# Edge-gated graph layer: one look-ahead tile, edge sums in pairs, z kept in used-up sums, products spread over a block

## The chip, the core and the metric

The kernel runs on one core of one Trainium2 chip. Its time is the device time of one launch in microseconds; the number compared is the median over several runs. All data is float32. Engines are named as the profile names them: PE (matrix products; PEld are its weight loads), DVE (vector), ACT (scalar and activation), POOL (here it only issues indirect transfers), SP (issues plain transfers).

## The reference, cut to what matters

```python
B, N, D = 16, 1024, 256                 # batches, nodes, features
pre_u = x @ W1[:D]                      # (B, N, D), per source node u
pre_v = x @ W1[D:]                      # (B, N, D), per target node v
hidden = relu(pre_u[:, :, None, :] + pre_v[:, None, :, :] + b1)      # (B, u, v, D)
S   = sigmoid(hidden @ W2 + b2)         # (B, u, v), one gate for each pair
a_t = einsum('buv,bud->bvd', S * adj, x)        # gated sums over the sources
m_t = einsum('uv,bud->bvd', adj, x) * x         # plain sums, times x
z   = x + (a_t @ Wa + ba) + (m_t @ Wm + bm)     # beta1 = beta2 = beta3 = 1
```

`adj` is mostly zero: 9052 of its 1024 x 1024 entries are not, at most 19 in a column. Gates are needed only for those.

## The kernel before, in words

**Edges, tiles, steps.** The kernel lists the edges and works on them alone. The 16 batches form 4 groups g of GB = 4; the 1024 targets form 8 tiles vt of 128. A pair (g, vt) is a *block*, 32 in all (`order`). A block has two windows w of 64 targets, and each window's edges lie in TW = 5 *edge tiles* j of up to 128 edges, one on each partition. So a block has T = 10 steps and the kernel 320; step n handles edge tile n, and s = n mod 10 is its place in the block. Targets of a window form four quarters of 16; edge tile j holds edges of one quarter (j = 0, 4) or of two (j = 1, 2, 3) (`QUARTERS`).

**What a tile needs.**
- `fetch(n)` (L494-499): POOL issues an indirect transfer which brings for each of the 128 edges the row of its source node from `table[g]`: 8 KB, the 4 x 256 values of pre_u and the 4 x 256 values of x. It goes into buffer `fetched[n % 6]`.
- `expand(n)` (L564-570): PE multiplies a 0/1 matrix (`marks`) with pre_v + b1 (`cuts`), which gives each edge the row of its target: 128 x 1024 in PSUM, tile `pc`, two buffers.
- `gate(n)` (L598-612): DVE adds both into the SBUF tile `t`, one buffer (L601); four DVE instructions, one for each batch, take relu, multiply by W2 and sum (L606); ACT makes the sigmoid (L609) and four copies (L612) that scale the one-hot adjacency columns by the gate. They fill the gated half of `lefts[n]`.
- `left_adj(n + 1)` (L573-580): ACT writes the ungated half of the next tile's `lefts`, a copy for each of the four batches.
- `aggregate(n)` (L614-625): PE multiplies `lefts` with the fetched x (L623). Each product uses 32 columns of the array, 16 targets gated and 16 ungated, and four batches fill 128. It adds up in `acc0` and `acc1`. `half_end` copies a finished pair of quarters to SBUF with ACT (L631).

**What a block needs besides.** `halves` (L452-468): pre_v of the next block on PE (L427, L431), its split into high and low parts on ACT and DVE (L461-468). `rows` (L434-446): pre_u of a block on PE, which SP writes to `table`. Group 0's table is made before the loop, the others inside it, each ahead of the group's use; the last `rows` are at step 233. `turn_over` (L633-657): transposes the sums on PE (L641), copies them on ACT into `LT` (L644), and two steps later DVE multiplies the ungated half by x (`times_h`, L654). `block_end` (L659-680): four pieces of products with Wa and Wm (L672), ACT copies them to `z` (L675), DVE adds x two steps later (L676), SP sends `z` out three steps after the last piece (L678). `lists(vt)` makes the edge lists; four of eight run inside the loop, their DVE instructions strewn between the gates by `fill`.

**Order.** All five queues are written by hand (`manual_schedule`): the order of the calls in the loop is the order on each engine, and the framework adds only the semaphore waits. `after(step, f)` puts f into a table that `do(step)` empties. A step before is, in this order:

```python
aggregate(n - 1); fetch(n - 1 + NF)            # NF = 6
gate(n); left_adj(n + 1)
do(n)
expand(n + 2)
# then transfers, lists, and the products of the block:
#   turn_over at s = 7 (two), 9, and 1 of the next block; block_end at s = 3, 4, 5, 6
#   halves at s = 0, 2, 3, 5, 6; rows by a table of steps (mostly s = 8 and 1)
```

Of the kernel before, what the change touches and what calls it, by code (L numbers as in the profile page):

```python
# [7 lines left out]
FP = mybir.dt.float32  # L8
# [5 lines left out]
P = 128  # L14
# [3 lines left out]
def kernel(  # L18
# [196 lines left out]
    wk = main.enter_context(tc.tile_pool(name="wk", bufs=3))  # L215
    psc = main.enter_context(tc.tile_pool(name="psc", bufs=2, space=bass.MemoryType.PSUM))
# [12 lines left out]
    NF = 6  # L229
# [9 lines left out]
    def lists(vt):  # L239
        key = fetched[vt + 1][:, :N] if vt < EARLY else big.tile([P, N], FP, name="key", bufs=1)  # L240
        (nc.sync if 2 <= vt < EARLY else nc.gpsimd).dma_start(key, adjT[vt * P:(vt + 1) * P, :])
        yield "load"
        R = wk.tile([P, RC], FP, name="R", bufs=4)
        top = R[:, 5:5 + S]
        count = wk.tile([P, 1], FP, name="count", bufs=4)
        unread = one.tile([P, N], mybir.dt.uint8, name="unread")
# [9 lines left out]
        cand = wk.tile([P, N // P, 8], FP, name="cand", bufs=2)  # L256
# [5 lines left out]
        cut = wk.tile([P, 1], FP, name="cut", bufs=2)  # L262
# [12 lines left out]
        used = wk.tile([P, S], FP, name="used", bufs=4)  # L275
# [14 lines left out]
        from_ = wk.tile([P, 1], FP, name="from", bufs=4)  # L290
# [9 lines left out]
        held = wk.tile([P, 1], FP, name="held", bufs=4)  # L300
# [10 lines left out]
        mark = big.tile([P, E], FP, name="made", bufs=1)  # L311
        nc.vector.tensor_scalar(mark, slot, R[:, 0:1], None, ALU.is_lt)
        yield "op"
        none = wk.tile([P, 1], FP, name="none", bufs=4)
# [6 lines left out]
        last = wk.tile([P, 1], FP, name="last", bufs=4)  # L321
# [4 lines left out]
        RR = wk.tile([P, NW, RC], FP, name="RR", bufs=2)  # L326
        few = wk.tile([P, E], mybir.dt.uint8, name="few", bufs=2)
# [13 lines left out]
        L = wk.tile([P, M, RC], FP, name="L", bufs=2)  # L341
# [3 lines left out]
        s_of = wk.tile([P, M], FP, name="s_of", bufs=2)  # L345
        nc.vector.tensor_tensor(s_of, slot_of.rearrange("p w j -> p (w j)"), L[:, :, 1], ALU.subtract)
        yield "op"
        eq = wk.tile([P, M, S], FP, name="eq", bufs=1)
# [5 lines left out]
        k_of = wk.tile([P, M], FP, name="k_of", bufs=2)  # L354
# [139 lines left out]
    def fetch(n):  # L494
        k, g, vt, w, j = where(n)
        nc.gpsimd.indirect_dma_start(  # L496
            out=fetched[n % NF], out_offset=None, in_=table[g],
            in_offset=bass.IndirectOffsetOnAxis(ap=uidx[:, vt * NW + w, j:j + 1], axis=0),
            bounds_check=N - 1, oob_is_err=False)
# [73 lines left out]
    def left_adj(n):  # L573
# [4 lines left out]
        lefts[n] = wk.tile([P, 2, GB, 2, V], FP, name="left")  # L578
        nc.scalar.activation(lefts[n][:, :m, :, 0, :], onehot[:, i, o:o + m, :].unsqueeze(2).to_broadcast([P, m, GB, V]),  # L579
# [17 lines left out]

    def gate(n):  # L598
        k, g, vt, w, j = where(n)
# [344 lines left out]
```

## Time and profile before

| | us |
|---|---|
| median of 3 runs (1163.63, 1163.78, 1171.99) | 1163.78 |
| the profiled execution: span | 1165.8 |
| first tile's DVE add (L601) starts | 71.6 |
| step 110 starts, by the same line | 480.8 |
| step 240 | 897.6 |
| step 319, the last | 1145.4 |
| busy in the span: PE / DVE / ACT / POOL | 1092.1 / 1056.2 / 893.5 / 439.9 |

A step starts here where DVE starts its add. The profiled execution is one of its own; it is 2 us longer than the median. PE's busy time is made of modelled ends of pipelined products, so what PE can spare is read from the distances between the starts of its products. The transfer engines (16, shared by all queues) move 391 MB in the span, 300 MB of it the indirect fetches.

### The profile page before, as it was taken

The page shows a single profiled execution, that of the slowest core. Times are in us where ns is not written, and L with a number is a line of the kernel's source. Part 1 is how long each engine was busy: PE and PEld are TensorE (multiplying, and loading weights), DVE is VectorE, ACT ScalarE, POOL GpSimd, SP SyncE. Part 2 cuts the span into 40 slices and gives each one's busy share as a digit, 9 for nine tenths or more (in the row PEclk, how much of TensorE's full clock was granted, in tenths as well). Part 3 has the DMA queues.
Part 4 walks back from the last instruction along what each step waited for, and adds up shares of the span by engine and source line. Part 5 has one row for each costly group of instructions (what it writes and reads, how often), then busy time and mean ns, then how long its engine had stood idle before and what let it go on. Part 6 is the DMA issues. An engine that isn't in the chain of part 4 may idle for free. (4 is left out here: it accounts for less than half of the span.)

```text
span 1165.8 us, 23918 instructions
## 1 busy us (share of the span) xinstructions
PE 1092.1 (94%) x7633; PEld 723.1 (62%) x7633; DVE 1056.2 (91%) x3487; ACT 893.5 (77%) x2624; POOL 439.9 (38%) x428
## 2 busy tenths in 40 slices
PE   7867899999999999999999999999999999999986
PEld 6744666666666666666666666666666666666553
DVE  7688889888999989999999999999999999999994
ACT  2346587767887878888888888888888888888873
POOL 1556645253335333443333333333333333333330
PEclk9868899999999999999999999999999999999999
DMA  9986898999999999999999999999998998999991
GB/s 286 298 307 223 277 372 312 362 320 331 342 320 323 396 379 336 358 350 402 389 374 369 355 364 356 360 364 383 371 375 324 361 322 333 334 339 328 328 346 60
DMA packets 147048, 391.40 MB, mean 336 GB/s; under 512 B 16753, under 2 KB 105329, under 8 KB 110705
## 3 DMA queue, kind: packets, MB, share of 16 engines
q0 software_dynamic: 50016, 300.50, 68.9%
q1 hardware_dynamic: 81616, 74.99, 20.0%
q10 hardware_dynamic: 15280, 14.29, 3.7%
q8 instruction: 63, 1.03, 0.3%
q14 instruction: 73, 0.59, 0.1%
HBM read 393.78 MB, written 50.33 MB: 381 GB/s over the span
## 5 line engine op out<-in xcount | busy, mean ns | idle before, releaser
L496 POOL DMA_INDIRECT fetched<-table,uidx x320 | 341.5, 1067 | 628.3 <-PE acc L623 447.2
L606 DVE SCALAR_TENSOR_TENSOR t<-t,w_b 128x256 f32<-128x256 f32 x1280 | 478.3, 421 | 19.3 <-ACT left L612 0.5
L601 DVE TENSOR_TENSOR t<-fetched,pc 128x1024 f32<-128x1024 f32 x320 | 389.3, 1217 | 41.4 <-PE pc L569 13.9
L623 PE MATMUL acc<-fetched,left 128*32 128x256 f32 x4096 | 336.2, 391 | 31.9 <-ACT left L612 26.2
L612 ACT ACTIVATE left<-left,gt 128x32 f32<-128x32 f32 (+1 forms) x1280 | 299.3, 304 | 10.4
L569 PE MATMUL pc<-X,mark 128*128 128x512 f32 x640 | 237.6, 453 | 6.2 <-ACT mark L562 5.0
L623 PEld LDWEIGHTS acc<-fetched,left 128*32 128x32 f32 x4096 | 130.6, 109 | 179.3 <-issue 52.4
L569 PEld LDWEIGHTS pc<-X,mark 128*128 128x128 f32 x640 | 97.2, 191 | 140.0 <-issue 89.3
L609 ACT ACTIVATE gt<-sc,b_b 128x4 f32<-128x4 f32 x320 | 96.2, 301 | 43.4 <-DVE t L606 40.8
L672 PE MATMUL misc<-w_m,LT 128*128 128x256 f32 x496 | 117.2, 379 | 0.0
L672 PE MATMUL misc<-w_a,LT 128*128 128x256 f32 x496 | 117.1, 379 | 0.0
L579 ACT ACTIVATE left<-onehot,val 128x128 f32<-128x128 bf16 (+1 forms) x320 | 116.5, 364 | 0.0
L427 PE MATMUL misc<-w_v,hT 128*128 128x256 f32 x448 | 107.3, 383 | 0.0
L427 PE MATMUL misc<-w_u,hT 128*128 128x256 f32 x416 | 101.2, 390 | 5.7 <-ACT few L329 3.6
L606 DVE DVE_READ_ACCUMULATOR t<-t,w_b 128x1 f32 x1280 | 104.0, 81 | 0.0
L672 PEld LDWEIGHTS misc<-w_a,LT 128*128 128x128 f32 x496 | 93.9, 189 | 15.1
L672 PEld LDWEIGHTS misc<-w_m,LT 128*128 128x128 f32 x496 | 93.8, 189 | 14.9
L382 POOL DMA_INDIRECT val<-in_adjT_dram,vidx x80 | 85.7, 1071 | 35.1 <-issue 22.4
L427 PEld LDWEIGHTS misc<-w_v,hT 128*128 128x128 f32 x448 | 86.0, 192 | 13.9
L427 PEld LDWEIGHTS misc<-w_u,hT 128*128 128x128 f32 x416 | 79.5, 195 | 17.3 <-ACT few L329 3.7
L631 ACT COPY ev<-acc 128x512 f32<-128x512 f32 x128 | 75.5, 590 | 14.6 <-PE acc L623 4.2
L675 ACT COPY z<-misc 128x512 f32<-128x512 f32 x62 | 36.3, 586 | 58.1 <-PE misc L672 38.8
(164 smaller groups left out, 947.9 us busy)
## 6 DMA issues: line engine op xcount, KB each, us to landing
h_blk<-in_x_dram SPq DMA_DIRECT2D x31, 512.0 KB
out_dram<-z SPq DMA_DIRECT2D x31, 512.0 KB
hT<-in_xT_dram SPq DMA_DIRECT2D x28, 512.0 KB
table<-in_x_dram ACTq DMA_DIRECT2D x24, 512.0 KB
table<-tab SPq DMA_DIRECT2D x24, 512.0 KB
fetched<-table,uidx POOLq DMA_INDIRECT x320
table<-in_x_dram SPq DMA_DIRECT2D x8, 512.0 KB
table<-fetched SPq DMA_DIRECT2D x8, 512.0 KB
```

Of the source, the lines that this page charges most:

```text
L382: nc.gpsimd.indirect_dma_start(out=val[:, i, j:j + 1], out_offset=None, in_=adj_flat, in_offset=bass.IndirectOffsetOnAxis(ap=vidx[:, i, j: ...
L427: nc.tensor.matmul(p[:, bb * D:(bb + 1) * D], hT[:, 2 * h + bb, i, :], wt[:, i, :], start=(i == 0 and not begun), stop=(i == DC - 1), skip ...
L496: nc.gpsimd.indirect_dma_start(out=fetched[n % NF], out_offset=None, in_=table[g], in_offset=bass.IndirectOffsetOnAxis(ap=uidx[:, vt * NW ...
L569: nc.tensor.matmul(pcs[n][:, c], marks[n // TW][:, j * P:(j + 1) * P], cuts[k][:, w, c], start=True, stop=True)
L579: nc.scalar.activation(lefts[n][:, :m, :, 0, :], onehot[:, i, o:o + m, :].unsqueeze(2).to_broadcast([P, m, GB, V]), AF.Copy, scale=val[:, ...
L601: nc.vector.tensor_tensor(t, fetched[n % NF][:, :GD].rearrange("p (b d) -> p b d", b=GB), pcs.pop(n).rearrange("p (b d) -> p b d", b=GB), ...
L606: nc.vector.scalar_tensor_tensor(t[:, b, :], t[:, b, :], 0.0, w2_b, ALU.max, ALU.mult, accum_out=sc[:, b:b + 1])
L609: nc.scalar.activation(gt, sc, AF.Sigmoid, bias=b2_b)
L612: nc.scalar.activation(lefts[n][:, :m, b, 1, :], lefts[n][:, :m, b, 0, :], AF.Copy, scale=gt[:, b:b + 1])
L623: nc.tensor.matmul(accs[h][b * 2 * V:(b + 1) * 2 * V, r, :], left[:, i, b].rearrange("p k v -> p (k v)"), f[:, GD + b * D:GD + (b + 1) * D ...
L631: nc.scalar.copy(evs[q], accs.pop(q))
L672: nc.tensor.matmul(pz[:, bb * D:(bb + 1) * D], LTs[k][:, c, 2 * h + bb, i, :], wt[:, c, :], start=False, stop=(i == 0 and c == DC - 1), sk ...
```

## The change

- **Add ahead.** The DVE add is a function of its own, `add(n)`, and is issued a step early: step n issues `add(n + 1)`, then `gate(n)`. The sum goes into the first half of the fetched buffer itself; the tile `t` is gone.
- **Aggregate later, in pairs.** Step n issues `aggregate(n - 2)`. From step 110 on, even steps issue none and odd steps issue those of n - 3 and n - 2 one after the other. The last steps catch up.
- **Buffers.** Seven fetch buffers in place of six, and an eighth from step 110 on, when the tiles of the edge lists (now in a pool of their own, `lst`) are given back. A fetch takes whichever buffer became free first. `lefts` has five buffers in place of three, each smaller: the ungated columns are written twice in place of four times, each copy shared by two neighbouring batches, so that in batches 1 and 3 the ungated 16 columns come first.
- **z.** The tile `z` is gone. ACT copies the products into the part of `LT` that they have just used up, DVE adds into the loaded x block (`h_blk`) one step later in place of two, and SP sends `h_blk` out. The next block's `h_blk` has the same single buffer. `times_h` of the second window comes one step after its transposes, not two.
- **Products spread.** The transposes stand at s = 8, 9, 0, 2, and `rows` mostly at s = 8 and 9. Up to step 119 `expand(n + 2)` and the products of the block are issued ahead of `add` and `gate`, from step 120 on after them.

The diff, cut to its core:

```diff
-    NF = 6
+    NF = 7
+    at_slot, free = {}, list(range(NF))
...
+        at_slot[n] = free.pop(0)
         nc.gpsimd.indirect_dma_start(
-            out=fetched[n % NF], out_offset=None, in_=table[g],
+            out=fetched[at_slot[n]], out_offset=None, in_=table[g],
...
-        lefts[n] = wk.tile([P, 2, GB, 2, V], FP, name="left")
-        nc.scalar.activation(lefts[n][:, :m, :, 0, :], onehot[:, i, o:o + m, :].unsqueeze(2).to_broadcast([P, m, GB, V]),
+        lefts[n] = wk.tile([P, 2, 2 * GB - 1, V], FP, name="left", bufs=5)
+        nc.scalar.activation(lefts[n][:, :m, 1::GB, :],
+                             onehot[:, i, o:o + m, :].unsqueeze(2).to_broadcast([P, m, GB // 2, V]),
...
+    def add(n):
+        t = fetched[at_slot[n]][:, :GD]
+        nc.vector.tensor_tensor(t, t, pcs.pop(n), ALU.add)
+
     def gate(n):
-        t = one.tile([P, GB, D], FP, name="t")
-        nc.vector.tensor_tensor(t, fetched[n % NF][:, :GD].rearrange("p (b d) -> p b d", b=GB),
-                                pcs.pop(n).rearrange("p (b d) -> p b d", b=GB), ALU.add)
+        t = fetched[at_slot[n]][:, :GD].rearrange("p (b d) -> p b d", b=GB)
...
-        after(step + (1 if k == BS - 1 else 2), times_h)
+        after(step + (1 if k == BS - 1 or w else 2), times_h)
...
-            nc.scalar.copy(z[:, sl], pz.rearrange("p (b d) -> p b d", b=2))
-            after(step + 2, lambda sl=sl: nc.vector.scalar_tensor_tensor(z[:, sl], hb[:, sl], be1, z[:, sl],
-                                                                         ALU.mult, ALU.add))
-        after(step + 3, lambda: nc.sync.dma_start(
-            out[g * GB:(g + 1) * GB, vt * P:(vt + 1) * P, :].rearrange("b p d -> p b d"), z))
+            z = LTs[k][:, 2 * h].rearrange("p k c n -> p (k c n)").rearrange("p (b d) -> p b d", b=2)
+            nc.scalar.copy(z, pz.rearrange("p (b d) -> p b d", b=2))
+            after(step + 1, lambda sl=sl, z=z: nc.vector.scalar_tensor_tensor(hb[:, sl], hb[:, sl], be1, z,
+                                                                              ALU.mult, ALU.add))
+        after(step + 2, lambda: nc.sync.dma_start(
+            out[g * GB:(g + 1) * GB, vt * P:(vt + 1) * P, :].rearrange("b p d -> p b d"), hb))
...
-        if 1 <= n <= total:
-            aggregate(n - 1)
-            fetch_val(2)
-            if n - 1 + NF < total:
-                fetch(n - 1 + NF)
...
+    ROOM, MORE = 110, 1
+    ahead = NF
+    add(0)
+    def refill():
+        nonlocal ahead
+        while free and ahead < total:
+            fetch(ahead)
+            ahead += 1
+    def gather_in(n):
+        aggregate(n)
+        free.append(at_slot.pop(n))
+        fetch_val(2)
+        refill()
+        if (n + 1) % TW in (0, MID + 1):
+            half_end(n, 0 if (n + 1) % TW else 1)
+    done = 0
+    for n in range(total + 2):
+        k, s = divmod(n, T)
+        if n < total - 3:
+            last_in = n - 1 if n % 2 or n < ROOM else done
+        else:
+            last_in = n
+        while done < min(last_in, total):
+            gather_in(done)
+            done += 1
...
+        if n < 120:
+            if n + 2 < total:
+                expand(n + 2)
+            products(n, k, s)
+        if n + 1 < total:
+            add(n + 1)
+        if n < total:
+            gate(n)
+            if n + 1 < total:
+                left_adj(n + 1)
+        do(n)
+        if n >= 120 and n + 2 < total:
+            expand(n + 2)
...
+        if n >= 120:
+            products(n, k, s)
+        if n == ROOM:
+            lists_done()
+            more = main.enter_context(tc.tile_pool(name="more", bufs=1))
+            for i in range(MORE):
+                free.append(len(fetched))
+                fetched.append(more.tile([P, 2 * GD], FP, name=f"fetched{len(fetched)}"))
+            refill()
```

## The prediction

> **What bounds the kernel now.** I read the sums by stage first, cut where the work changes: up to about step 110 edge lists are made between the gates, up to about step 235 tables are built, after that neither.
>
> ```profile
> core 0: us, PE busy (x) PEld busy (x) DVE busy (x) ACT busy (x) POOL busy (x), PEclk, DMA share, GB/s
> 72.00:480.00 408.00, 381.86 (x2604) 253.25 (x2606) 367.72 (x1255) 307.27 (x900) 181.58 (x173) 0.97 0.92 329
> 480.00:890.00 410.00, 406.52 (x2934) 268.19 (x2926) 387.46 (x1218) 344.21 (x1027) 148.85 (x138) 1.00 0.99 368
> 890.00:1140.00 250.00, 239.87 (x1722) 152.00 (x1719) 239.77 (x758) 208.15 (x633) 82.70 (x80) 1.00 0.92 334
> ```
>
> Restricted to line L601, the same view counts 110, 128 and 80 adds, so a step takes 3.71, 3.203 and 3.125 us in stages A, B and C. No engine is idle for long: PE 94 to 99% busy, DVE 90, 94.5 and 96%, transfers 92 to 99%. Three candidates; each needs its own floor.
>
> *DVE.* The timeline of DVE for a few steps (start, duration, instruction) shows what the busy share hides.
>
> ```profile
> 702.76 0.74 DVE L676 SCALAR_TENSOR_TENSOR z<-h_blk,be,z 128x512 f32<-128x512 f32 x1
> 703.43 1.21 DVE L601 TENSOR_TENSOR t<-fetched,pc 128x1024 f32<-128x1024 f32 x1
> 704.67 0.42 DVE L606 SCALAR_TENSOR_TENSOR t<-t,w_b 128x256 f32<-128x256 f32 x1
> 705.03 0.08 DVE L606 DVE_READ_ACCUMULATOR t<-t,w_b 128x1 f32 x1
> 705.03 0.42 DVE L606 SCALAR_TENSOR_TENSOR t<-t,w_b 128x256 f32<-128x256 f32 x1
> ...
> 708.96 0.42 DVE L606 SCALAR_TENSOR_TENSOR t<-t,w_b 128x256 f32<-128x256 f32 x1
> 709.30 0.08 DVE L606 DVE_READ_ACCUMULATOR t<-t,w_b 128x1 f32 x1
> 709.47 1.22 DVE L601 TENSOR_TENSOR t<-fetched,pc 128x1024 f32<-128x1024 f32 x1
> ```
>
> Independent neighbours overlap: L676 lasts 0.74, yet L601 starts 0.67 after it; gates follow each other every 0.345 though each lasts 0.42. The first gate after an add reads what the add wrote and starts only 1.24 after it (mean of 600 to 900 us: 1.285; where an independent list instruction follows the add it is 1.138). And an add right behind a gate (46 of 94 steps there) starts 0.17 after the last accumulator read, because `t` has one buffer. So a step of DVE is 1.285 + 4 x 0.345 + 0.49 x 0.17 + a tenth of the block's other work (2 x 0.664 for L676, 2 x 0.604 for L654, 1.137 for L463, together 3.67) = 3.115. Stage C's 3.125 is this: there DVE is the bound.
>
> *PE.* In 600 to 900 us the starts of products leave no hole, 3.19 us a step. But some of it is waiting. A tile with one quarter goes from its first L623 product to the next operation in 0.569 at best, a mean of 0.622; one with two quarters in 1.000 and 1.189 (250 to 1100 us): 0.4 x 0.053 + 0.6 x 0.189 = 0.135 a step, spent on scaled columns that ACT has not finished.
>
> ```profile
> PEld pc L569 <- issue: 89.3, 215, 0.8
> ...
> PEld acc L623 <- ACT left L612: 50.7, 87, 3.9
> ```
>
> These lines of the waits (total, times, longest) show that wait in the second row, and in the first another: a hole before the 128-column load of L569 on every change from the 32-column products. By starts, L623 to L569 is 0.309 against 0.216 between equal products, the two L569 are 0.335 apart against 0.230 from the second to what follows, and entering L623 costs 0.309 against 0.216: 0.30 a round trip.
>
> *Transfers.* DVE waited for a fetch only 2.8 us in all:
>
> ```profile
> DVE t L601 <- DMA fetched<-table,uidx: 2.8, 3, 1.7
> ```
>
> So transfers are not the bound yet, but stage B moves 368 GB/s at a share of 0.99. In stretches of 2 us with at least 0.8 fetches outstanding, 383 GB/s flow in that stage. At that rate a step of B is 3.203 x 368 / 383 = 3.08. Those of A and C, at a share of 0.92, are 3.41 and 2.87.
>
> **The change, part by part.** The sum is made against the profiled span, 1165.8, which is 2.0 above the median.
>
> *Add ahead, in place.* No instruction is added on DVE; both stalls go. `add(n + 1)` is followed by gates of tile n, whose sum is a step old, and no shared `t` stands between. The new step is 1.138 + 1.38 + 0.367 = 2.885, 0.23 less. Bounds: 0, if an add still holds what follows it for its full 1.22 plus the wait (the row of L606 as it is), and 0.23, the rows of independent neighbours. I take 0.23, since L601 followed by an unrelated list instruction is this very case. In stage A up to half of the adds have that already, so 0.1 to 0.2.
>
> The Trainium skill, page "VectorE: DVE Perf Modes", section "The DRAIN you can't avoid", speaks against this: chaining without semaphores saves nothing, "the semaphore costs nothing extra here". This trace disagrees (1.285 against 1.138). By the page the saving on DVE would be 0 and the new time about 1140, from what PE gains alone.
>
> *Aggregate later.* PE's products for tile n - 2 find columns that ACT finished about a step before, so PE's 0.135 goes; what is late next is the fetch buffer, freed a step later. It is paid with the seventh buffer. The lead of a fetch, from the end of gate n - 2 to the add of n + 5, is five steps as before. By packet starts and mean rows a fetch lands 5.3 to 6.9 us after its issue (means of 20 steps) and 2.5 to 7.3 before its add, so one step less would cost a wait in the worst stretches; I see none less. POOL's queue holds nothing but fetches (and list values up to about step 40), so a late one holds only the next.
>
> *Pairs from step 110.* Half of the round trips go: 0.30 / 2 = 0.15 a step. PE's step becomes 3.19 - 0.135 - 0.15 = 2.90, on a level with DVE. Two fetches are issued together, and the eighth buffer gives the second one six steps.
>
> *Smaller parts.* Half the ungated copies: ACT's L579 has 64 in place of 128 elements in most tiles, at most 0.364 - 0.291 = 0.07 us of an engine that is 77 to 84% busy; costed at 0, hidden behind DVE. z through `LT`: the same ACT copies and DVE instructions; `z` saved only space. SP gets a new wait: the next `h_blk` load must see the last output land; behind it stand an hT load and, later, a table write. They are needed 5 and 8 steps later (15 and 24 us), against a landing within some 7 us as fetches show; 0, and if that cover failed, about a step (3 us) in each of 31 blocks. Products spread: the same PE work; two transposes no longer stand in one step; between -0.05 and +0.05 a step, taken as 0. Start and tail (71.6 and 20.4 us) keep their work: 0, within 3 us.
>
> *Sum.* C: floors 2.885 (DVE), 2.87 (transfers), PE lower since no `rows`; with 0.05 of waits 2.935, so 80 x 0.19 = -15. B: 3.08 (transfers), 2.90, 2.885; I take 3.09: 128 x 0.113 = -14.5. A: PE waits (13.9 us of holes, 24.1 at loads) and DVE stalls shrink, PE at its lower clock early on, transfers allow 3.41; half of that way, 3.56: 110 x 0.15 = -16.5. Together -46: a span of 1119.8, a median of 1118. Bounds: A -2 to -33, B 0 to -32 (2.95, were transfers no bound), C -8 to -19: 1156 to 1082.
>
> The page "DMA: Bandwidth & Descriptors", section "Where 436 GB/s comes from", gives about 358 GB/s as a core's share of its memory, so B would have nothing left. The row, 368 on average and 383 with a backlog, is already above it; by the page the sum would lose B's 14.5 and be about 1132.
>
> **The rivals.**
>
> *Transfers take over everywhere.* Everything DVE and PE give back becomes waiting for fetches. For it: 0.99 in B, and slices of the page at 1.0 of busy. Against it: 2.8 us of waits in all, and A and C at 0.92. Then B gains 0, A -5, C -10: about 1149, on the edge of what a measurement of this kernel tells from no change, about 1%.
>
> *DVE's floor is reached.* If the share of 0.99 is packets waiting on each other, not capacity, B goes to 2.95 and A to 3.41: -32 - 33 - 15, about 1084. For it: stretches of 7.5 us with over 410 GB/s in the transfer view. Against it: three engines at 2.9 with different bursts seldom mesh.
>
> *DVE waits for z.* The x addition (two a block) now comes one step behind its products, and `times_h` too. If PE runs behind DVE by more than the 1.4 us of four gates, DVE stands still, where the second step of slack covered it. A piece of products takes 8 x 0.216 = 1.73 and ACT's copy 0.59: up to 2.3 us for each of 62 additions, 143 us. For it: ACT already waits 38.8 us for those products (`z` L675). Against it: DVE waited for `z` 0.5 us in all, and after step 120 PE has the add's product out ahead of the piece. With PE fully late the time is 1118 + 143 = 1261; from 0.75 us an addition the change is lost.
>
> That the change doesn't do what it says I give nothing: the built program's order shows pairs and the early add.
>
> **How the numbers follow.** Forecast 0.62; DVE's floor 0.14; transfers 0.14, half of it within 1%; waits for z 0.10. Faster by over 1%: 0.62 + 0.14 + 0.07 = 0.83; within 1%: 0.07; slower: 0.10. The range runs from 1092, most of the way to DVE's floor, to 1156; it leaves out the slow rival and a part of the fast one.
>
> **What would show it.** Right: the first gate no longer 1.24 behind an add, and adds followed by the next instruction after 1.14; C near 2.94 a step, B near 3.09; `acc` <- ACT left small; holes before L569's load halved in number after step 110; DVE waiting some tens of us for fetches in B. Wrong: adds still hold DVE for 1.24; DVE waits for `z` or `LT` by tens of us; B unchanged with fetch waits to match; or A unchanged, its bound being none of these.

## The result, and the profile after

The changed kernel takes 1232.74 us (median of 4 runs, 1225.72 to 1239.63) against 1164.57 (4 runs, 1163.63 to 1171.99) for the kernel before: a ratio of 1.055, 95% interval 1.049 to 1.061. It is slower, where the forecast said 1118 and gave a slower outcome one chance in ten.

The sums by stage of the kernel after, cut at steps 0, 110, 240 and 319 (columns as in the prediction):

```profile
core 0: us, PE busy (x) PEld busy (x) DVE busy (x) ACT busy (x) POOL busy (x), PEclk, DMA share, GB/s
71.00:488.00 417.00, 378.99 (x2580) 249.16 (x2583) 356.99 (x1243) 299.28 (x893) 181.85 (x173) 0.97 0.92 322
488.00:963.00 475.00, 414.98 (x3009) 289.73 (x3001) 380.10 (x1247) 346.05 (x1051) 152.38 (x142) 0.92 0.88 323
963.00:1206.00 243.00, 220.86 (x1691) 148.12 (x1691) 227.65 (x751) 198.03 (x621) 79.72 (x75) 0.97 0.91 333
```

By DVE's adds the stages took 417.2, 474.5 and 243.3 us, against 409.2, 416.7 and 247.8 before. So the loss is in B: +58 us, with PE down to 87% busy (it was 99%). A is 8 us worse, C only 4.5 better; the rest (start and end) adds 3.6.

In the kernel after, the add is L606, the gates L614, the expansion L574, the edge sums L631 and ACT's copies for them L619; transposes L649 and their copy L652; the copy of z L684, the addition of x L685, the output L687, the `h_blk` load L855; `hT` load L420, row products L431, copy to `tab` L447, table write L450.

Three of the forecast's signs came true. DVE's timeline after step 240 (start, duration, instruction):

```profile
990.29 1.21 DVE L606 TENSOR_TENSOR fetched<-fetched,pc 128x1024 f32<-128x1024 f32 x1
991.42 0.41 DVE L614 SCALAR_TENSOR_TENSOR fetched<-fetched,w_b 128x256 f32<-128x256 f32 x1
...
992.80 0.08 DVE L614 DVE_READ_ACCUMULATOR fetched<-fetched,w_b 128x1 f32 x1
992.80 1.21 DVE L606 TENSOR_TENSOR fetched<-fetched,pc 128x1024 f32<-128x1024 f32 x1
```

The gate starts 1.13 after the add, not 1.24, and the next add starts with the last accumulator read: both stalls are gone. And among the waits (us in total, times, longest)

```profile
PE misc L431 <- DMA hT<-in_xT_dram: 31.6, 5, 8.4
...
PEld pc L574 <- issue: 50.6, 119, 1.0
...
PEld acc L631 <- ACT left L619: 26.8, 26, 4.3
...
DVE fetched L606 <- PE pc L574: 114.7, 48, 9.8
...
DVE fetched L606 <- DMA fetched<-table,uidx: 6.6, 3, 3.7
```

the holes ahead of the expansion's load fell from 89.3 to 50.6 us, and PE's loads wait half as long for ACT's columns (50.7 before). The other rows are new: DVE stands 114.7 us for the expansion (13.9 before), PE itself stands for `hT` (two more rows, of single `hT` tiles, add 3.5 and 3.1 us), and fetches, for which the forecast expected some tens of us, are not the cause (6.6 us).

The chain of waits shows where PE stands (start, length, what):

```profile
535.11 25.40 DMA hT<-in_xT_dram
...
560.64 3.56 PE misc L431 x8
...
568.93 0.59 ACT tab L447
569.51 0.20 ACT gt L617
569.72 0.16 SPq L450
...
569.93 0.52 SPq L855
...
570.54 29.97 DMA hT<-in_xT_dram
...
600.65 3.75 PE misc L431 x8
```

Read from below: the first row product of a block (L431) waits for an `hT` load that took 30 us. SP issued it at 570.54, after the table write (L450), which stood for ACT's copy into `tab`, and after the `h_blk` load (L855). This is a ring: the load, the row products, ACT's copy, the table write and the next load. Here it takes 35.4 us from one `hT` issue to the next (535.11 to 570.54), about a block of this stretch.

PE pays a second time behind each hole. The eight row products that the wait held back take 3.65 us, the next eight 1.70, and the clock column says why (stretch, its length, PE busy, PEld busy, granted clock, share, GB/s; line L431 alone):

```profile
600.65:604.30 3.65, 3.65 (x8) 2.50 (x8) 0.50 0.07 23
607.50:609.20 1.70, 1.70 (x8) 1.26 (x8) 1.00 0.91 226
```

The waits of SP's own queue, first in the kernel before, then after:

```profile
SPq L678 <- DVE z L676: 638.1, 30, 30.9
SPq L446 <- ACT gt L609: 250.3, 20, 52.3
```

```profile
SPq L450 <- ACT gt L617: 317.1, 23, 46.8
SPq L687 <- DVE h_blk L685: 276.9, 23, 20.6
SPq L687 <- DMA h_blk<-in_x_dram: 268.8, 26, 19.2
SPq L855 <- DMA out_dram<-h_blk: 72.1, 13, 12.9
```

Before, SP waited mostly for z, and for the copy that a table write needs. For most tiles of the last group both stand at s = 9, four steps of the program ahead of the `hT` load at s = 3. SP then ran on at once through the `h_blk` load and the `hT` load, and issued an `hT` about 11 steps ahead of its use. After, the table write stands at s = 0, directly in front of the `h_blk` and `hT` loads of the same step; the `hT` load is issued about 5.6 steps, 17 us, ahead, and takes 25 to 30. In B, PE has a hole of 3.1 to 8.4 us where the first row product of each block stands: ten holes from step 130 to 220, together 50.8 us. The profile puts seven of them (38.2 us) down to the `hT` load and three to ACT. The slow products behind the ten holes, 3.0 to 3.8 us in place of 1.89 from first start to last end, add 17 us. That is more than the 58 us that B lost, so by PE's time the rest of B gained.

### The profile page after: what moved, and what is told of

Same layout as the page of the kernel before. It is cut to its first block, busy times and chain, and to the rows that moved or that the text cites. A ratio compares the mean times of both kernels' runs of the same rounds, so it can differ in the third digit from the quotient of the medians.

```text
span 1230.6 us, 23771 instructions
## 1 busy us (share of the span) xinstructions
PE 1075.2 (87%) x7633; PEld 734.8 (60%) x7633; DVE 1022.3 (83%) x3487; ACT 874.8 (71%) x2624; POOL 441.2 (36%) x428
## 3 DMA queue, kind: packets, MB, share of 16 engines
q1 hardware_dynamic: 81616, 74.99, 19.1%
## 4 chain that ended last, share of the span: by engine, by line
PE 41%; DMA 24%; DVE 19%; ACT 8%; issue 7%; ACTq 1%; another core or an unknown queue 0%; SPq 0%; POOL 0%; DVEq 0%; POOLq 0%
PE misc L431 14%; DMA hT<-in_xT_dram 11%; PE acc L631 10%; DVE fetched L614 9%; PE pc L574 6%; DVE fetched L606 6%; PE misc L680 5%; DMA out_dram<-h_blk 3%; DMA h_blk<-in_x_dram 3%; DMA hT__6552<-in_xT_dram 2%; DMA hT__6925<-in_xT_dram 2%; PE misc L649 2%; ACT left L619 2%; PE misc L435 1%; DMA table<-tab 1%
## 5 line engine op out<-in xcount | busy, mean ns | idle before, releaser
L606 DVE TENSOR_TENSOR fetched<-fetched,pc 128x1024 f32<-128x1024 f32 x320 | 388.4, 1214 | 150.6 <-PE pc L574 114.7
L614 DVE SCALAR_TENSOR_TENSOR fetched<-fetched,w_b 128x256 f32<-128x256 f32 x1280 | 475.0, 417 | 0.0
L631 PE MATMUL acc<-fetched,left 128*32 128x256 f32 x4096 | 297.2, 395 | 22.4 <-ACT left L619 15.5
L619 ACT ACTIVATE left<-left,gt 128x32 f32<-128x32 f32 (+1 forms) x1280 | 299.5, 304 | 10.4
L574 PE MATMUL pc<-X,mark 128*128 128x512 f32 x640 | 233.1, 456 | 13.9 <-DVE fetched L606 8.4
L631 PEld LDWEIGHTS acc<-fetched,left 128*32 128x32 f32 x4096 | 126.1, 112 | 160.5 <-issue 56.2
L574 PEld LDWEIGHTS pc<-X,mark 128*128 128x128 f32 x640 | 104.7, 192 | 112.3 <-issue 50.6
L431 PE MATMUL misc<-w_u,hT 128*128 128x256 f32 x416 | 115.5, 430 | 53.1 <-DMA hT<-in_xT_dram 31.6
L431 PEld LDWEIGHTS misc<-w_u,hT 128*128 128x128 f32 x416 | 86.3, 216 | 68.7 <-ACT LT L652 25.5
L431 PE MATMUL misc<-w_v,hT 128*128 128x256 f32 x448 | 111.7, 394 | 0.0
L584 ACT ACTIVATE left<-onehot,val 128x64 f32<-128x64 bf16 (+1 forms) x320 | 102.9, 321 | 0.0
L614 DVE DVE_READ_ACCUMULATOR fetched<-fetched,w_b 128x1 f32 x1280 | 101.7, 79 | 0.0
L431 PEld LDWEIGHTS misc<-w_v,hT 128*128 128x128 f32 x448 | 89.4, 200 | 13.0
L649 PE MATMUL misc<-ident,ev 128*128 128x128 f32 x512 | 79.8, 279 | 13.3 <-ACT ev L639 8.5
```

Of the source, the lines that this page charges most:

```text
L431: nc.tensor.matmul(p[:, bb * D:(bb + 1) * D], hT[:, 2 * h + bb, i, :], wt[:, i, :], start=(i == 0 and not begun), stop=(i == DC - 1), skip ...
L574: nc.tensor.matmul(pcs[n][:, c], marks[n // TW][:, j * P:(j + 1) * P], cuts[k][:, w, c], start=True, stop=True)
L584: nc.scalar.activation(lefts[n][:, :m, 1::GB, :], onehot[:, i, o:o + m, :].unsqueeze(2).to_broadcast([P, m, GB // 2, V]), AF.Copy, scale=v ...
L606: nc.vector.tensor_tensor(t, t, pcs.pop(n), ALU.add)
L614: nc.vector.scalar_tensor_tensor(t[:, b, :], t[:, b, :], 0.0, w2_b, ALU.max, ALU.mult, accum_out=sc[:, b:b + 1])
L619: nc.scalar.activation(lefts[n][:, :m, 2 * b, :], lefts[n][:, :m, 1 + b // 2 * GB, :], AF.Copy, scale=gt[:, b:b + 1])
```

## The experiments

Ratios are to the kernel before on the same chip, with a 95% interval. A profile is one execution, and executions of a changed kernel lie up to 2.5% apart, so stage times serve as illustration and the ratios decide. The four kernels from ht_early to before_new_table ran on a chip where the kernel before takes 1148 us (1165 to 1172 for the others), so their stage times are some 1.5 to 2% low beside the other rows. Stages by DVE's adds, in us:

| kernel | ratio | A: 0-110 | B: 110-240 | C: 240-319 |
|---|---|---|---|---|
| before | 1 | 409.2 | 416.7 | 247.8 |
| after | 1.055 [1.049, 1.061] | 417.2 | 474.5 | 243.3 |
| ht_early | 1.017 [1.012, 1.022] | 409.4 | 421.3 | 243.3 |
| old_table | 1.016 [1.012, 1.020] | 398.4 | 417.7 | 244.9 |
| tab_later | 1.031 [1.024, 1.037] | 412.1 | 429.9 | 240.5 |
| before_new_table | 1.033 [1.026, 1.040] | 404.6 | 440.9 | 247.2 |
| no_pairs | 1.000 [0.996, 1.004] | 418.1 | 413.0 | 233.6 |
| expand_first | 0.999 [0.996, 1.003] | 421.5 | 419.9 | 233.9 |
| hblk_alt | 1.015 [1.008, 1.022] | 418.9 | 421.6 | 240.6 |
| add_ahead | 1.012 [1.008, 1.016] | 414.6 | 426.8 | 249.6 |
| late_products | 1.007 [1.004, 1.011] | 430.0 | 418.5 | 232.5 |
| late_expand_first | 1.005 [1.002, 1.007] | 424.8 | 422.2 | 236.6 |
| unspread | 1.006 [1.003, 1.008] | 414.3 | 425.5 | 240.5 |
| before_again | - | 409.8 | 416.6 | 247.6 |
| add_from_110 | 1.000 [0.997, 1.003] | 417.9 | 428.6 | 232.5 |
| early_as_before | 0.992 [0.989, 0.996] | 410.2 | 419.4 | 234.3 |
| expand_first_single | 0.997 [0.994, 1.000] | 414.9 | 424.7 | 234.0 |
| rows_together | 0.998 [0.996, 1.001] | 412.8 | 413.2 | 233.0 |
| pairs_behind | 1.001 [0.998, 1.004] | 418.2 | 420.8 | 236.4 |
| two_h_blk | 0.984 [0.979, 0.988] | 419.7 | 402.6 | 232.7 |

### Is it the table's order that makes hT late?

Four kernels, each one edit away from after or from before. In the plan table a line is (step of the `hT` load, steps of the two row products).

```diff
 # ht_early: after, loads of the last two groups six steps sooner
-        plan([(g, vt) for vt in range(NT)], ((first + 10 * i, first + 8 + 10 * i, first + 9 + 10 * i)
+        plan([(g, vt) for vt in range(NT)], ((first - 6 + 10 * i, first + 8 + 10 * i, first + 9 + 10 * i)
 # old_table: after with the plan lines of before; before_new_table: before with those of after
 # tab_later: after, and in rows()
-        after(step + 1, lambda: nc.sync.dma_start(table[g][nt * P:(nt + 1) * P, :GD], tab))
+        after(step + 2, lambda: nc.sync.dma_start(table[g][nt * P:(nt + 1) * P, :GD], tab))
```

> The changed kernel with one edit: the hT loads that feed the table rows of groups 2 and 3 stand 6 steps earlier on SP's queue (14 and 15 steps ahead of their two products, in place of 8 and 9). Theory 1, late hT: in the changed kernel SP issues hT about 2.4 steps after its place in the program, behind a table write that waits for ACT and an h_blk load that waits for the last output to land; the transfer then takes 24 to 30 us and PE stands still for it in every block of steps 120 to 220. With 6 steps more, the wait is covered: blocks of stage B go from 34.5-40 us to about 31, time 1150 to 1180. Rival 1, PE's pairs make the expand product late and DVE waits for it whatever the loads do: stays above 1215. Rival 2, a deeper backlog of fetches starves the plain transfers, so that any load comes late: the transfer takes longer still, recovery less than half, above 1200.

> The changed kernel with the whole table of steps for hT loads and table rows as it was before (loads of group 3 mostly at s = 3, rows at s = 1 and 8), all else changed. Theory 1: SP has the table write out of the way before the h_blk and hT loads, hT is issued 8 or more steps before its use as before, time 1150 to 1180. Rival 1 (pairs): above 1215. Rival 2 (backlog): above 1200.

> The changed kernel with one number changed: the table write stands one step later on SP's queue, so that at s = 0 the h_blk and hT loads stand ahead of it and not behind it. Theory 1 with the table write as the main cause: hT is issued some 2 steps earlier, most of the loss comes back, 1165 to 1195. Theory 1 with the wait of h_blk for the landing of the output as the main cause: hT moves by less than a step, above 1205. Rival 1: no change, 1225 to 1240.

> The kernel before with one part of the change alone: the new table of steps for hT loads and table rows (loads at s = 0, rows at s = 8 and 9). SP's table write then stands ahead of the h_blk and hT loads, but h_blk has no output to wait for, since z is a tile of its own. Theory 1: hT has about 6.5 steps (21 us) for a transfer of 18 to 29 us, so some blocks wait: 1175 to 1205. Rivals 1 and 2: the new table costs nothing without pairs and the deeper backlog, 1160 to 1170.

An earlier load alone, and the old table alone, take the ratio from 1.055 to 1.017 and 1.016, and B from 474.5 to 421 and 418 us; PE's wait for `hT` in B is gone in one and down to 1.8 us in the other. So 3.8 of the 5.5% are the late `hT`, by two edits that have nothing else in common. The new table alone, put on the kernel before, costs 3.3%: it needs none of the other parts, and so not SP's new wait for the output either (there `z` is a tile of its own, and the `h_blk` load waits for no output). Letting only the table write come a step later, behind the `hT` load in SP's order, takes away 2.4%, with 12.0 us of PE's wait for `hT` in B left. What the change made worse is the issue, not the transfer: by its packets, an `hT` load of the last group took 18 to 30 us in the kernel before too.

### Do the pairs stand in the way of the expansion?

From step 110 on both sums of a pair stand on PE ahead of `expand(n + 2)`, which DVE wants one gate later.

```diff
 # no_pairs: old_table, sums one by one, no eighth buffer
-            last_in = n - 1 if n % 2 or n < ROOM else done
+            last_in = n - 1
-    ROOM, MORE = 110, 1
+    ROOM, MORE = 110, 0
 # expand_first: old_table with pairs, from step 120 on ahead of the sums
+        if n >= 120 and n + 2 < total:
...
+            expand(n + 2)
         while done < min(last_in, total):
             gather_in(done)
```

> The changed kernel with the old table of steps (as in old_table) and without pairs: every step issues aggregate(n - 2), seven fetch buffers throughout. Theory 2, the pair stands ahead of the expand product on PE's queue and DVE waits for that product (45 us of waits of L606 for L574 in old_table after step 120): those waits fall under 20 us, ratio to the kernel before 0.99 to 1.01 against 1.016 with pairs. Rival: pairs save PE's round trips as forecast, so that without them PE is slower by 0.15 us a step after step 110, 30 us, ratio 1.03 to 1.045.

> The changed kernel with the old table of steps, pairs kept, and from step 120 on expand(n + 2) issued on PE's queue ahead of the pair and not behind it. Theory 2: DVE's waits for L574 mostly go, blocks after step 240 come to 29.7 us each (the DVE floor seen in some of them) and those of 120 to 240 to 30 to 31.5; ratio 0.975 to 1.0. Rival, PE lacks throughput and not order: DVE's waits stay within a third, ratio 1.01 to 1.02.

DVE's wait for the expansion after step 120, in old_table, in no_pairs and in expand_first:

```profile
DVE fetched L606 <- PE pc L574: 44.2, 31, 4.1
```

```profile
DVE fetched L606 <- PE pc L574: 18.4, 33, 1.2
```

```profile
DVE fetched L606 <- PE pc L574: 14.7, 20, 2.9
```

Both edits take 1.6 to 1.7% off, and the blocks of stage C go from 29.7 and 31.3 in turn to a steady 29.4 and 29.0. The last is 2.90 a step, close to DVE's floor of 2.885. So it is the place of the pairs, not the pairs; but in the better place they bring nothing either over single sums (0.999 against 1.000).

### Does SP's wait for h_blk cost anything by itself? Is C bound by DVE?

```diff
 # hblk_alt: old_table, two h_blk tiles in turn after step 110
-            hbs[k - 1] = big.tile([P, GB, D], FP, name="h_blk", bufs=1)
+            hbs[k - 1] = (more if n > ROOM and k % 2 else big).tile([P, GB, D], FP, name="h_blk", bufs=1)
 # add_ahead: before, with the add of the change and nothing else
+        if n + 1 < total:
+            add(n + 1)
         if n < total:
             gate(n)
```

> The changed kernel with the old table of steps and, after step 110, two h_blk buffers in turn, so that SP's h_blk load does not wait for the last output to land. Theory 3, the in-place x block costs through SP's queue: the tail gets back its 3 to 4 us and some loads come earlier, 4 to 10 us less than old_table, ratio 1.006 to 1.013. Rival: the wait is covered, no change, 1.014 to 1.018.

> The kernel before with one part of the change alone: the DVE add a step early and in place in the fetched buffer, still six fetch buffers, aggregation of n - 1 as before. If the two DVE stalls (0.23 us a step by the forecast) are real and DVE is the bound, stage C goes from 31.3 us a block to 29.5 to 30.5 and the ratio is 0.975 to 0.995. Rival 1: a fetch now has a step less before its add, DVE waits for fetches by tens of us, ratio 1.0 to 1.03. Rival 2: PE and its waits for scaled columns set the pace, ratio 0.995 to 1.005.

hblk_alt, at 1.015 [1.008, 1.022], is where old_table is, at 1.016: at this pace the wait is covered, as far as these intervals tell (0.8% could hide in them). (At a faster pace it is not; see the last two kernels.) In add_ahead both of DVE's stalls are gone, and yet C's blocks stay at 31.3 us, and the kernel is 1.2% slower. DVE has a new wait in place of its stalls:

```profile
DVE fetched L600 <- PE pc L569: 80.1, 106, 4.4
```

An expansion stands on PE behind the sums of n - 1. Those wait for ACT's columns, which wait for the gates; with the add a step early the expansion is wanted one gate sooner. In steps 240 to 314 of add_ahead 50 of 75 adds start within 0.2 us of the end of their expansion. (Fetches, one step later for their add with six buffers, cost DVE another 19.1 us in all, but only 1.2 of it from 940 to 1145 us.) So C is held there by that loop through all three engines. In the kernel before it is not: DVE's only waits of over 0.15 us from 898 to 1145 are

```profile
DVE t L601 <- DMA fetched<-table,uidx: 0.6, 1, 0.6
DVE t L606 <- ACT left L612: 0.5, 1, 0.5
```

and the expansion was done 2.7 us ahead of its add (the median). There DVE is the bound, stalls included; that the loop came out at the same 31.3 us a block is chance as far as these runs show. It takes the later sums and the early add together (no_pairs) to bring C to 29.4.

### Where did A's gain go?

```diff
 # late_products: no_pairs with the order of the steps from 120 on used from step 0
 # late_expand_first: the same done to expand_first
 # unspread: late_products with turn_over at s = 7 (two), 9, 1, as in before
 # add_from_110: late_products, add(n) in its own step up to 110
+        if n <= ROOM:
+            add(n)
+        if ROOM <= n < total - 1:
+            add(n + 1)
 # early_as_before: add_from_110 with turn_over as in unspread up to step 110
 # expand_first_single: early_as_before, expand(n + 2) ahead of aggregate after step 110
```

> The plan table of before, sums one by one (as in no_pairs), and the order of a step that the change uses from step 120 on is used from step 0: the products of the blocks and the table come behind the gates and the expansion, as in the kernel before. In no_pairs the steps 0 to 110 took 418.1 us against 409.2 in the profile of before, and in that stretch VectorE stood 36.6 us for PE's expansion (L574) against 9.3 and ScalarE's copies for X and the table stood 52 us for PE against 26. Theory: the order, which puts the products ahead of the expansion's users for the first 120 steps, makes this wait; without it steps 0 to 110 take 408 to 411 us, VectorE's wait for L574 falls below 15 us, and the ratio to before falls from 1.000 to 0.992 to 0.994. Rival: the wait belongs to the add that stands a step ahead (the expansion is wanted a step earlier whatever the order): steps 0 to 110 stay at 416 to 420 us, the wait above 30 us, the ratio 0.999 to 1.002.

> As late_products, but with the edge sums in pairs from step 110 and PE's expansion ahead of them (as in expand_first) in all steps. Theory (the two costs are separate and add): steps 0 to 110 as in late_products (408 to 411 us), blocks of 29.0 us after step 240 as in expand_first, and no stretch of 38 us at steps 110 to 120, since the order no longer changes at step 120: ratio 0.985 to 0.990. Rival: the 38 us stretch belongs to the pairs' start and the slow first stage to the add ahead; both stay, ratio 0.998 to 1.002.

> late_products with the transposed sums turned over where the kernel before has them (both of the first half at s = 7, the first of the second at s = 9, the last at s = 1) in place of one at each of s = 8, 9, 0, 2. Theory, the forecast's: spreading them is worth nothing, since in either place some engine works without a gap: within 0.3% of late_products. Rival: eight transposes and two copies in one step make VectorE and the gates wait once in each block: 0.3 to 0.5 us in each of 31 blocks, 9 to 15 us, 0.8 to 1.3% above late_products.

> The kernel before, unchanged, for the times of its stages in a second execution: steps 0 to 110, 110 to 240, 240 to 319 took 409.2, 416.7 and 247.8 us in the profile of before. Theory: each is within 4 us of that, so that the 418 us of steps 0 to 110 in no_pairs are a loss by the change. Rival: the first stage differs that much from one execution to the next, and is 415 us or more here too.

> late_products, but the add of a step's tile stands in its own step up to step 110, as in the kernel before, and only then a step ahead. Theory: the add a step ahead is what costs time in the first 110 steps. It wants the expansion of a tile one gate earlier, while that expansion stands on PE behind the edge sums, which wait for the gates two steps back. Without it VectorE's wait for L574 in this stretch falls from 40 us to below 15 us, the stretch takes 408 to 413 us in place of 430, and with blocks as in no_pairs after it the ratio to before is 0.985 to 0.990. Rival: the stretch is slow for another reason (the spread products, or the place of z), and stays at 420 us or more, ratio 1.000 or above.

> As add_from_110, and up to step 110 the transposed sums are turned over where the kernel before has them, so that of the change only the reuse of buffers is left in that stretch. Theory: 405 to 411 us for it, and 0.983 to 0.990 for the ratio. Rival: if add_from_110 is as fast as this, the spread of the products has no part in the first stretch; if only this one is fast, it has. If both stay above 418 us, the cause is neither.

> As early_as_before, with the expansion ahead of the edge sums on PE after step 110, the sums one by one. Theory: VectorE's last waits for the expansion go, the blocks after step 240 come down from 29.4 to 29.0 us as in expand_first, those of steps 110 to 240 stay at 31.4 us, where PE works without a gap: 3 us less than early_as_before, 0.2 to 0.3%. Rival: without pairs, the sums then stand behind an expansion that waits for an add, and PE stands in turn: the blocks after step 110 become longer by 0.5 us or more, ratio 1% above early_as_before.

The kernel before repeats its stages within 1 us, and the kernel after and three of its kin (no_pairs, expand_first, hblk_alt) all take 417 to 422 us, so A's loss is real. The order is not its cause: late_products and late_expand_first are no better than their models (1.007 and 1.005), and the theory put there falls. The early add has a part: in add_from_110 DVE's wait for the expansion in A falls from 40.4 to 5.0 us. But another takes its place, the mechanism of the rival "DVE waits for z", since the addition of x now comes one step behind its products (in the kernel after itself DVE never waits for that copy in A):

```profile
DVE h_blk L685 <- ACT LT L684: 26.0, 14, 4.9
...
DVE fetched L606 <- PE pc L574: 5.0, 4, 2.0
```

The spread has two signs. Undone everywhere (unspread), the blocks after step 240 take 30.3 us in place of 29.4 and most of those before 32.6 in place of 31.4, since PE comes to the transposes before ACT has copied the sums:

```profile
PEld misc L649 <- ACT ev L639: 36.2, 29, 2.4
```

but A is shorter in its profile, and the ratio is the same, 1.006 against 1.007. Undone up to step 110 only (early_as_before), it brings 0.8%, from 1.000 to 0.992: faster than before. What holds A beyond that I can't say: the sums a step later, the buffers and z's new place are left of the change there, and DVE still waits 16.4 us for z's copy. The five kernels whose first 110 steps are the same as those of early_as_before (it and the four after it) took 410 to 420 us there, none below the kernel before; so for the changed kernels one profile of A is good to some 10 us, no better.

expand_first_single is slower than early_as_before (0.997). DVE's waits for the expansion fall from 33.7 to 16.5 us in all. But after step 110 those for fetches rise from 4.2 to 13.3, as a sum that stands later frees its buffer later, and those for z's copy (L685 <- L684) from 0.4 to 15.2. What helped the pairs does not help single sums.

### What still makes single blocks long?

early_as_before has one block of 37.9 us among blocks of 31.4. Its profile names the cause there:

```profile
781.10 0.59 ACT L447 COPY tab<-misc 128x512 f32<-128x512 f32 x1 [4.86 <-DMA table<-tab]
```

The table write had been issued at 768.04; ACT may not overwrite `tab` before it has landed, 13 us later, and gates and sums stand behind ACT's copy. The new table leaves `tab` alone for nearly a block; the fault found in it was the late `hT`. So both are put right together, and then the pairs come back, and then the second `h_blk` tile:

```diff
 # rows_together: early_as_before, and for the last group
+    plan([(3, vt) for vt in range(NT)], ((134 + 10 * i, 148 + 10 * i, 149 + 10 * i) for i in range(NT)))
 # pairs_behind: rows_together with pairs and the eighth buffer from 110 on, and expand(n + 2) ahead of the sums
 # two_h_blk: pairs_behind with the edit of hblk_alt
```

> early_as_before, with the table's last eight tiles planned as the change has them (the two row products at s = 8 and 9 of one block, so that the staging tile tab is free for nearly a block before it is written again) and their hT loads 14 steps ahead, as in ht_early. In early_as_before block 20 took 37.9 us in place of 31.4: ScalarE stood 4.9 us for the table write to land before it could copy into tab, and PE and VectorE stood behind it. Theory: such blocks of 35 us and more after step 110 come from that wait; without it steps 110 to 240 take 408 to 412 us in place of 419, and the ratio to before is 0.981 to 0.988. Rival: a late landing only moves on to the next transfer in SP's queue (the hT load or the h_blk load), the long blocks stay, ratio 0.990 to 0.996.

> rows_together, with the edge sums in pairs from step 110 on, as in the change, but behind PE's expansion. It asks what the pairs themselves are worth once hT and tab are no longer late. The forecast's price: 0.15 us a step less on PE, and so 1.5 us a block less where PE works without a gap (steps 110 to 240), 20 us in all, and 29.0 us a block at the end: ratio 1.5 to 2% below rows_together. Rival, by the blocks of expand_first: 30.8 us in place of 31.4 there and 29.0 in place of 29.4 after, 0.6 x 13 + 0.4 x 8 = 11 us at most, and less where the sums of a pair bring PE and VectorE out of step: 0 to 0.9% below, or above it.

> pairs_behind with two tiles for h_blk that take turns after step 110, so that its load no longer waits on SP for the output of the block before to land. In pairs_behind the load went out at 793.5 us, some two steps after its place, and VectorE stood 5.6 and 6.9 us for it in the two blocks looked at, 24.7 us in 6 waits in all, with every engine behind it. Theory: the wait that the forecast priced at nothing costs this once the sums run at full pace; without it the long blocks go, steps 110 to 240 take 395 to 405 us, and the ratio to before is 0.975 to 0.988. Rival: as in hblk_alt, where the same edit moved nothing, another transfer (the table write, hT) is late next; VectorE's waits for h_blk go, PE's or ScalarE's for hT or tab come, and the ratio stays at 0.995 to 1.003.

rows_together has no block over 33.7 us after step 110 in its profile, but that was its fastest execution (1154.8 of 1154.8 to 1179.1), and at 0.998 the theory's 0.981 to 0.988 is missed. What makes its other executions longer is not known, as only this one has a profile. pairs_behind is no faster (1.001): its usual block in B is 29.8 to 30.5 us, but six take 33 to 36. DVE's wait, and one case of it in DVE's timeline (line numbers behind the loop have moved: the load is L861 here):

```profile
DVE h_blk L685 <- DMA h_blk<-in_x_dram: 24.7, 6, 6.9
```

```profile
808.29 0.75 DVE L685 SCALAR_TENSOR_TENSOR h_blk<-h_blk,be,LT 128x512 f32<-128x512 f32 x1 [6.91 <-DMA h_blk<-in_x_dram]
```

SP had issued that load at 793.53, 14.8 us earlier. SP's own wait in front of it, in pairs_behind and in two_h_blk:

```profile
SPq L861 <- DMA out_dram<-h_blk: 170.6, 23, 17.8
```

```profile
SPq L861 <- DMA out_dram<-h_blk: 77.2, 11, 14.6
```

With two tiles in turn two_h_blk reaches 0.984, 1.8% below pairs_behind by this one edit, and is the fastest of all: the waits of DVE for `h_blk` loads are gone, and its stages after step 110 are

```profile
491.00:894.00 403.00, 388.95 (x2968) 275.91 (x2972) 378.23 (x1233) 342.35 (x1041) 149.29 (x141) 0.99 1.00 377
894.00:1126.00 232.00, 213.16 (x1706) 142.76 (x1698) 227.50 (x750) 199.24 (x619) 83.21 (x76) 0.99 0.94 350
```

Five things set it apart from the change: up to step 110 the add in its own step, and the transposes in their old places; the products behind the gates throughout, with the expansion ahead of the pairs after step 110; the plan table; and the second `h_blk` tile. Which of them it could do without was not tried; the second tile on the single sums of rows_together, for one, was not.

## Why the prediction was wrong, by its own steps

**The step that failed** is the paragraph on the smaller parts, in two terms put at 0. The first is "Products spread: the same PE work ... taken as 0". Spreading the rows also moved the table write on SP's queue, from four steps ahead of the `hT` load to directly in front of it. The load keeps its 8 steps of lead in the program, but its real lead fell from 11 steps to 5.6, 17 us, and that had no price. The second is the cover itself: "They are needed 5 and 8 steps later (15 and 24 us), against a landing within some 7 us as fetches show; 0". The 7 us is the landing of a fetch, 128 rows of 8 KB on POOL's queue. SP's transfers are 512 KB in smaller packets, and the runs show 13 us for a table write, 14.8 for an `h_blk` load and 25 to 30 for `hT`. Together the two cost 3.8% (old_table, ht_early).

The wait that the prediction did name, of the `h_blk` load for the last output, was not what failed first. It put the table write behind that wait; in the changed kernel the write stands in front. old_table keeps the wait and is rid of the 3.8%; before_new_table has no such wait and loses 3.3%; hblk_alt takes it away and gains nothing clear of noise. Its price of 0 broke only at the faster pace of pairs_behind, where it costs 1.8%. That its price for a failed cover, about a step in each of 31 blocks (95 us), lies nearer to the +58 us of B than 0 does is luck: the cover that failed was another.

**PE's order.** "Pairs from step 110" were priced by what they save, 0.15 us a step, not by what they stand in front of: 1.6% for DVE's wait behind them. In the usual block of B the saving is there: 29.8 to 30.5 us in pairs_behind against 31.4 without pairs (31.2 with the expansion ahead and no pairs), 0.09 to 0.16 a step.

**The sums for B and C hold once the covers are real.** Forecast were 3.09 us a step in B and 2.935 in C; two_h_blk has 402.6 / 130 = 3.10 and 232.7 / 79 = 2.95. In two_h_blk the fetches are no wall at 383 GB/s either: its shortest blocks of steps 140 to 230, 29.8 us, run at 2.98 a step, below the floor of 3.08, and move 390 to 399 GB/s. (The floors of A and C were scaled by the share of 0.92, B's by GB/s; scaled as B's they are 3.71 x 329 / 383 = 3.19 and 3.125 x 334 / 383 = 2.73.) C's reading, "there DVE is the bound", holds for the kernel before; what the sum left out is that the expansion must arrive earlier when the add does, which add_ahead shows. The later sums, in the same change, gave that time back.

**A** was forecast at -16.5. In the kernel after it is +8, and in the kernels compared later +1 to +21 (only the four of the first comparison, on a chip where the kernel before took 1148 us, lie at 398 to 412 us). Half of the distance to a floor was a guess, and its rows (stalls of DVE, waits of PE) were not traced to what would wait next. In the kernel after, that is DVE for the expansion: 30.9 us in A against 9.3 before.

**The products' spread**, priced at 0 within 0.05 a step, is worth 0.09 to 0.12 after step 110 by the blocks of unspread, and costs time before it: 0.8% by early_as_before, and as much as it is worth by unspread's equal ratio. **The end**, priced at 0, grew by 2.3 us, from 17.7 to 20.0 between the last gate and the end. **The rivals:** "DVE waits for z" does not explain the kernel after, where DVE waits 0 us for that copy; it shows in A in its variants, at up to 11 us with the early add and at 13 to 26 once the add is back in its own step, and not at 143. For the loss in B no rival had the mechanism.

## What to carry to other kernels

When a wait on an in-order queue is added or moved, price every transfer behind it with the landing time of that transfer's own kind under this kernel's load, and compare that with the lead that the issue really has in the trace, not with the steps in the program: two plans with the same 8 steps gave 11 and 5.6. A cover found at today's pace (hblk_alt) can be gone at a faster one (two_h_blk), so the same edit is worth trying again after the other stalls are removed. And where engines hand work round in a loop, a stall removed on one of them shows up on the next until the loop itself has been given slack.

## What the hardware showed that was not expected

An `hT` load of 512 KB needs 25 to 30 us beside the fetches. In the 30 us from 570.5 on, the packets in the trace are 1001 of 8 KB on POOL's queue, 312 ns each (the median), and 2955 of 512 or 1024 bytes on SP's, 27 and 46 ns each: SP's take a fifth of the engines' time. The load was not alone on its queue either: SP issued a table write, an `h_blk` load and two `hT` loads, 2 MB, between 569.54 and 571.72. How much of the 30 us is the neighbours on POOL's queue, and how much these, was not separated. The Trainium skill, page "DMA: Bandwidth & Descriptors", section "Queues, rings and completion order", says that each transfer engine takes turns between its queues, a packet at a time. Small packets slowed by large neighbours would agree with that, though a packet of the page groups several descriptors and the trace doesn't mark such groups; how strict the turns are, no run here shows.

The granted clock followed PE's standing: 0.92 in B after the change, 1.00 before, 0.99 in two_h_blk. In B after, it is made of twelve stretches at 0.5, each 3.4 to 10.2 us long, 78.5 us in all, nearly all of them at the holes; in B before there is none. The L631 products took 395 ns on average against 391 before, so they hardly show it. The row products right behind a hole do: 17 us in ten blocks.
